# A 3x3 convolution on images kept without a zero border: the centre tap writes every pixel, the other eight add only where a neighbour exists

## The chip, the core and the metric

The kernel runs on one core of a Trainium2 chip. The metric is device time in microseconds (us) of one execution. Before the change three runs gave 1373.08, 1372.49 and 1372.67 us, a median of 1372.67.

## What is computed

The input is 160 images of 128 channels by 32 x 32 pixels. Each image is group-normalised (32 groups of 4 channels), convolved with one of five quantised 3x3 weight sets, and added to itself.

```python
def reference(x, U):
    beta, alpha = jnp.max(U), jnp.min(U)
    s1 = (beta - alpha) / 3.0
    v1 = s1 * floor(U / s1)
    s2 = s1 / 5.0
    v2 = s2 * floor((U - v1) / s2)
    w = (v1 + v2).reshape(128 * 5, 128, 3, 3)
    xb = group_norm(x, groups=32, eps=1e-5).reshape(32, 5 * 128, 32, 32)
    act = conv(xb, w, stride=1, padding=1, feature_group_count=5)
    return x + act.reshape(x.shape)
```

So image 5b + n uses weight set n, and there are 32 images for each of the 5 sets.

## The kernel before

Channels lie on the 128 partitions; an image is one row of 1024 float32 values per partition. Images of one weight set are taken in groups of four (`NB`), one load and one store of 2 MB per group: 40 groups, 160 images. `load` (L288) issues the loads on SyncE's queue, three groups ahead; the stores are issued on ScalarE's queue (L359).

For one group, `statistics` calls `group_statistics` (L126): VectorE takes `bn_stats` of each half image (L135) and `bn_aggr` (L136), a tiny matmul with `gavg` averages over the four channels of a group (L139), VectorE makes the variance, a second tiny matmul averages that (L146), GpSimd raises it to the power -0.5 (L150), and VectorE scales the result (L152).

For one image, `split` (L298) makes the two float16 operands: VectorE normalises into `z` (L302), ScalarE rounds `z` to float16 as `hi` (L311), VectorE subtracts and writes the remainder as `lo` (L312). `hi` and `lo` go into the middle of a padded image of 34 x 34, whose border of zeros was written once: six pairs of such images exist, cleared by GpSimd at the start with 12 memsets (L268).

`conv` (L314) then runs 36 matmuls per image: 9 taps, times `hi` and `lo`, times the two halves of 16 rows. Each streams 16 rows of 32 pixels (512 columns) from the padded image, shifted by the tap, against that tap's 128 x 128 weights, and accumulates in a PSUM tile `pc` of two banks, one per half:

```python
r0 = h * HROWS + kh
nc.tensor.matmul(
    pc[:, h, :].rearrange("p (h w) -> p h w", w=W),
    wt[:, tap, :],
    pair[part][:, r0 : r0 + HROWS, kw : kw + W],
```

A row of the padded image has 34 float16 values (68 bytes), so a tap with `kw` = 1 starts every row on an odd element. VectorE then adds `pc`, scaled, to the image (L332).

`make_weights` (L274) quantises one weight set on VectorE in 17 passes over 1152 values (L87 to L93, L104, L105, L277), transposes the nine taps on TensorE in batches of 4, 4 and 1 (L284), and ScalarE copies each batch to float16 (L285). All quantising needs the global maximum and minimum of U: `Steps` reduces each set on VectorE (L39, L40), then across partitions on GpSimd (L44), and derives the steps in small VectorE operations that begin with `span` (L67).

No order is written out by hand: a scheduler in the framework places the instructions on each engine's queue from its own model of when things are ready, and each engine then runs its queue in that order.

Of the kernel before, what the change touches and what calls it, by code (L numbers as in the profile page):

```python
# [8 lines left out]
F32 = mybir.dt.float32  # L9
I32 = mybir.dt.int32  # L10
MM = mybir.dt.float16
ALU = mybir.AluOpType
# [5 lines left out]
TAPS = 9  # L18
EPS = 1e-5
NB = 4  # L20
# [89 lines left out]
def group_mean_matrix(nc, pool):  # L110

    P = nc.NUM_PARTITIONS
    gavg = pool.tile([P, P // GROUP, GROUP], F32, tag="gavg", name="gavg")
    nc.gpsimd.memset(gavg, 1.0 / GROUP)
    nc.gpsimd.affine_select(
        out=gavg, in_=gavg, compare_op=ALU.is_ge, fill=0.0, base=0,
        pattern=[[-GROUP, P // GROUP], [0, GROUP]], channel_multiplier=1,
    )
    nc.gpsimd.affine_select(
        out=gavg, in_=gavg, compare_op=ALU.is_ge, fill=0.0, base=GROUP - 1,  # L120
        pattern=[[GROUP, P // GROUP], [0, GROUP]], channel_multiplier=-1,
    )
    return gavg.rearrange("p g k -> p (g k)")
# [91 lines left out]
def main_path(tc, keep, x, u, out):  # L215

    nc = tc.nc
    IMGS, C, H, W = x.shape
    P = nc.NUM_PARTITIONS
    assert C == P and H * W == 1024
    PIX = H * W
    HALF = PIX // 2
    HROWS = H // 2  # L230
    FW = C * TAPS
    n_chunks = IMGS // (N_SETS * NB)

    xv = x.rearrange("(b n) c h w -> n c b (h w)", n=N_SETS)
    ov = out.rearrange("(b n) c h w -> n c b (h w)", n=N_SETS)
    uv = u.rearrange("n (o f) -> n o f", o=C)

    ctx = ExitStack()
    const = ctx.enter_context(tc.tile_pool(name="const", bufs=1))
    qpool = ctx.enter_context(tc.tile_pool(name="quant", bufs=1))  # L240
    xpool = ctx.enter_context(tc.tile_pool(name="x", bufs=4))
    zpool = ctx.enter_context(tc.tile_pool(name="z", bufs=2))
    small = ctx.enter_context(tc.tile_pool(name="small", bufs=3))
    ps_conv = ctx.enter_context(tc.tile_pool(name="ps_conv", bufs=3, space=PSUM))
    ps_stat = ctx.enter_context(tc.tile_pool(name="ps_stat", bufs=1, space=PSUM))
    ps_tr = ctx.enter_context(tc.tile_pool(name="ps_tr", bufs=1, space=PSUM))


    us = []
    for n in range(N_SETS):  # L250
        un = const.tile([P, FW], F32, tag=f"u{n}", name=f"u{n}")
        nc.scalar.dma_start(un, uv[n])
        us.append(un)

    ident = const.tile([P, P], F32, tag="ident", name="ident")
    make_identity(nc, ident)
    gavg = group_mean_matrix(nc, const)
    mhalf = const.tile([P, NB], F32, tag="mhalf", name="mhalf")
    nc.gpsimd.memset(mhalf, -0.5)


    N_PADS = 6
    pads = []
    for i in range(N_PADS):
        pair = []
        for part in ("hi", "lo"):
            pad = const.tile([P, H + 2, W + 2], MM, tag=f"{part}{i}", name=f"{part}{i}")
            nc.gpsimd.memset(pad, 0.0)  # L268
            pair.append(pad)
        pads.append(pair)  # L270

    steps = Steps(nc, keep, us)

    def make_weights(n):  # L274

        k1, k2, _ = steps.quantise(qpool, us[n], n)
        nc.vector.scalar_tensor_tensor(k2, k1, 5.0, k2, ALU.mult, ALU.add)  # L277
        wt = const.tile([P, TAPS, C], MM, tag=f"wt{n}", name=f"wt{n}")
        k3 = k2.rearrange("o (i k) -> o i k", k=TAPS)
        for t0 in range(0, TAPS, 4):  # L280
            cnt = min(4, TAPS - t0)
            pt = ps_tr.tile([P, 4, C], F32, tag="pt", name=f"pt{n}_{t0}")
            for k in range(cnt):
                nc.tensor.transpose(pt[:, k, :], k3[:, :, t0 + k], ident)  # L284
            nc.scalar.copy(wt[:, t0 : t0 + cnt, :], pt[:, :cnt, :])  # L285
        return wt

    def load(g):  # L288
        n, c = divmod(g, n_chunks)
        xt = xpool.tile([P, NB, PIX], F32, tag="xt", name=f"xt{g}")  # L290
        nc.sync.dma_start(xt, xv[n, :, c * NB : (c + 1) * NB, :])
        return xt

    def statistics(g, xt):
        images = [xt[:, j, :] for j in range(NB)]
        return group_statistics(nc, small, ps_stat, gavg, mhalf, images, SCALE, g)

    def split(g, j, xt, gm, rstd):  # L298

        hi, lo = pads[(g * NB + j) % N_PADS]  # L300
        z = zpool.tile([P, H, W], F32, tag="z", name=f"z{g}_{j}")
        nc.vector.tensor_scalar(  # L302
            z,
            xt[:, j, :].rearrange("p (h w) -> p h w", w=W),
            gm[:, j : j + 1],
            rstd[:, j : j + 1],
            ALU.subtract,
            ALU.mult,
        )
        hi_in = hi[:, 1 : H + 1, 1 : W + 1]  # L310
        nc.scalar.copy(hi_in, z)  # L311
        nc.vector.tensor_sub(lo[:, 1 : H + 1, 1 : W + 1], z, hi_in)  # L312

    def conv(g, j, xt, wt):  # L314


        pair = pads[(g * NB + j) % N_PADS]
        pc = ps_conv.tile([P, 2, HALF], F32, tag="pc", name=f"pc{g}_{j}")
        for tap in range(TAPS):
            kh, kw = divmod(tap, 3)  # L320
            for part in range(2):
                for h in range(2):
                    r0 = h * HROWS + kh
                    nc.tensor.matmul(  # L324
                        pc[:, h, :].rearrange("p (h w) -> p h w", w=W),
                        wt[:, tap, :],
                        pair[part][:, r0 : r0 + HROWS, kw : kw + W],
                        start=(tap == 0 and part == 0),
                        stop=(tap == TAPS - 1 and part == 1),
                    )  # L330
        xj = xt[:, j, :].rearrange("p (h f) -> p h f", h=2)
        nc.vector.scalar_tensor_tensor(xj, pc, steps.s2z, xj, ALU.mult, ALU.add)  # L332

    total = N_SETS * n_chunks
    ahead = 3
    xts = {g: load(g) for g in range(min(ahead, total))}
    wts = {0: make_weights(0)}
    norm = statistics(0, xts[0])
    split(0, 0, xts[0], *norm)
    split(0, 1, xts[0], *norm)  # L340
    for g in range(total):
        n, c = divmod(g, n_chunks)
        xt = xts.pop(g)
        for j in range(NB):

            if j == 1 and g + 1 < total:
                norm_next = statistics(g + 1, xts[g + 1])
            if j < 2:
                split(g, j + 2, xt, *norm)
            elif g + 1 < total:  # L350
                split(g + 1, j - 2, xts[g + 1], *norm_next)
            conv(g, j, xt, wts[n])
            if j == 0 and g + ahead < total:
                xts[g + ahead] = load(g + ahead)
            if j == 2 and c == 1 and n + 1 < N_SETS:
                wts[n + 1] = make_weights(n + 1)
        if g + 1 < total:
            norm = norm_next
        nc.scalar.dma_start(ov[n, :, c * NB : (c + 1) * NB, :], xt)  # L359
    ctx.close()  # L360
    return steps


@with_exitstack
def preact_conv_kernel(
    ctx: ExitStack,
    tc: tile.TileContext,
    x: bass.AP,
    u: bass.AP,
    out: bass.AP,  # L370
):

    keep = ctx.enter_context(tc.tile_pool(name="keep", bufs=1))
    steps = main_path(tc, keep, x, u, out)
    general_path(tc, keep, steps, x, u, out)
# [28 lines left out]
```

## Time and profile before

| what | us |
|---|---|
| median of 3 runs | 1372.67 |
| the profiled execution, its own time | 1372.45 |
| its span in the trace | 1370.7 |
| TensorE matmul busy | 1294.6 (94%) |
| VectorE busy | 851.3 (62%) |
| ScalarE busy | 168.5 (12%) |
| GpSimd busy | 58.4 (4%) |

A row of the timeline gives the start, the length, the engine, the line and how many instructions were merged; the distance between two starts is the firmer number for matmuls, whose ends are modelled. The table by stage gives each engine's busy time in a stretch. The chain is the sequence of work, each piece released by the one above it, that ended last.

### The profile page before, as it was taken

Reading aid. Unit: us, or ns where it says so; the run is one execution under the profiler, and the core shown is the slowest. Engines: PE = TensorE matmul, PEld = TensorE weight load, DVE = VectorE, ACT = ScalarE, POOL = GpSimd, SP = SyncE. Lnnn points to the kernel's source line nnn. Section 1 sums busy time; section 2 is a strip of 40 time slices with the busy share of each in tenths; the row PEclk is TensorE's granted clock in tenths of the full one; section 3 lists DMA queues with packets and bytes.
Section 4 is the critical chain, followed back from the end, with each engine's and each line's share of the span. In section 5 each row is a group of like instructions: output and inputs, shape, how many; then the busy total and the mean of one; then the engine's idle time right before and its main releaser. Section 6 shows DMA issues by size and latency. Waiting matters only on the chain.

```text
span 1370.7 us, 13928 instructions
## 1 busy us (share of the span) xinstructions
PE 1294.6 (94%) x5965; PEld 584.2 (43%) x5965; DVE 851.3 (62%) x1317; ACT 168.5 (12%) x176; POOL 58.4 (4%) x63
## 2 busy tenths in 40 slices
PE   0199999999999999999999999999999999999997
PEld 0044444444444444444444444444444444444443
DVE  7999975555597666656555555555666665555331
ACT  0201111111111111111111111111111111111110
POOL 4100000000000000000000000000000000000000
PEclk9999999999999999999999999999999999999999
DMA  8003333333433333333333333324333333333221
GB/s 331 0 0 123 123 137 150 143 128 126 174 121 128 123 123 123 123 124 123 123 123 138 150 143 128 152 113 161 123 124 123 123 123 124 123 123 134 89 84 64
DMA packets 43030, 171.69 MB, mean 125 GB/s; under 512 B 1360, under 2 KB 1360, under 8 KB 42960
## 3 DMA queue, kind: packets, MB, share of 16 engines
q1 hardware_dynamic: 21120, 83.89, 16.3%
q10 hardware_dynamic: 21840, 86.84, 15.4%
q8 instruction: 48, 0.79, 0.2%
q14 instruction: 22, 0.18, 0.0%
HBM read 86.84 MB, written 83.89 MB: 125 GB/s over the span
## 4 chain that ended last, share of the span: by engine, by line
PE 86%; DVE 12%; DMA 1%; POOL 0%; issue 0%; ACTq 0%; ACT 0%
PE pc L324 85%; DVE st L135 2%; DVE lo L312 2%; DVE xt L332 1%; DMA u<-in_L_conv_U_dram 1%; DVE z L302 1%; DVE tt L89 1%; DVE tt L91 1%; DVE tt L90 1%; DVE tt L92 1%; DVE k L93 1%; DVE nn L87 0%; DVE k L277 0%; DVE nn L88 0%; PE pg L146 0%; PE pt L284 0%
## 5 line engine op out<-in xcount | busy, mean ns | idle before, releaser
L324 PE MATMUL pc<-hi,wt 128*128 128x512 f16 x2880 | 870.4, 383 | 0.0
L324 PE MATMUL pc<-lo,wt 128*128 128x512 f16 x2880 | 870.3, 383 | 0.0
L324 PEld LDWEIGHTS <-wt 128*128 128x128 f16 x5760 | 561.4, 98 | 692.1 <-issue 2.1
L332 DVE SCALAR_TENSOR_TENSOR xt<-pc,s2z,xt 128x1024 f32<-128x1024 f32 x160 | 204.6, 1279 | 421.0 <-PE pc L324 421.0
L311 ACT CAST hi<-z 128x1024 f16<-128x1024 f32 x160 | 160.2, 1047 | 1079.3 <-DVE z L302 1064.7
L135 DVE BATCH_NORM_STATS2 st<-xt 128x6 f32<-128x512 f32 x320 | 200.5, 666 | 0.0
L312 DVE TENSOR_TENSOR lo<-z,hi 128x1024 f16<-128x1024 f32 x160 | 189.3, 1224 | 16.7 <-ACT hi L311 16.7
L302 DVE TENSOR_SCALAR z<-xt,gm,rstd 128x1024 f32<-128x1024 f32 x160 | 123.1, 809 | 1.3
L150 POOL TENSOR_TENSOR rstd<-ve,mhalf 128x4 f32<-128x4 f32 x40 | 44.1, 1103 | 1239.6 <-DVE ve L148 1230.2
L139 PE MATMUL pg<-mv,gavg 128*128 128x4 f32 x80 | 11.7, 217 | 27.7 <-DVE mv L136 25.9
L284 PE MATMUL pt<-ident,k 128*128 128x128 f32 x45 | 9.2, 318 | 29.6 <-DVE k L277 27.7
L152 DVE TENSOR_SCALAR rstd<-rstd 128x4 f32<-128x4 f32 x40 | 6.8, 170 | 41.9 <-POOL rstd L150 41.9
L136 DVE BATCH_NORM_AGGREGATE mv<-st 128x2 f32<-128x12 f32 x160 | 31.4, 196 | 0.0
L139 PEld LDWEIGHTS pg<-mv,gavg 128*128 128x128 f32 x80 | 15.4, 196 | 33.3 <-issue 25.9
L284 PEld LDWEIGHTS pt<-ident,k 128*128 128x128 f32 x45 | 7.0, 200 | 33.6 <-DVE k L277 27.8
L146 PEld LDWEIGHTS pg<-dv,gavg 128*128 128x128 f32 x80 | 13.9, 194 | 17.1 <-DVE dv L145 17.1
L146 PE MATMUL pg<-dv,gavg 128*128 128x4 f32 x80 | 12.3, 224 | 8.9 <-DVE dv L145 8.9
L148 DVE TENSOR_SCALAR ve<-pg 128x4 f32<-128x4 f32 x40 | 6.5, 162 | 18.3 <-PE pg L146 18.2
L92 DVE TENSOR_TENSOR tt<-tt,nn 128x1152 f32<-128x1152 f32 x10 | 13.5, 1355 | 0.1
L93 DVE TENSOR_TENSOR k<-nn,tt 128x1152 f32<-128x1152 f32 x10 | 13.4, 1345 | 0.1
L39 DVE TENSOR_REDUCE ext<-u 128x1 f32<-128x1152 f32 x5 | 6.8, 1353 | 6.9 <-DMA u<-in_L_conv_U_dram 6.9
L285 ACT CAST wt<-pt 128x512 f16<-128x512 f32 (+1 forms) x15 | 7.2, 479 | 27.4 <-PE pt L284 27.4
(53 smaller groups left out, 127.6 us busy)
## 6 DMA issues: line engine op xcount, KB each, us to landing
xt<-in_x_dram SPq DMA_DIRECT2D x40, 2048.0 KB, 7.5
out_dram<-xt ACTq DMA_DIRECT2D x40, 2048.0 KB, 6.4
u<-in_L_conv_U_dram ACTq DMA_DIRECT2D x5, 576.0 KB, 10.1
```

The source lines that it names most:

```text
L92: nc.vector.tensor_tensor(t, t, n, ALU.is_lt)
L93: nc.vector.tensor_sub(k, n, t)
L135: nc.vector.bn_stats(st[:, h, :], image[:, h * half : (h + 1) * half])
L136: nc.vector.bn_aggr(mv[:, j, :], st)
L139: nc.tensor.matmul(pg[:, 0, :], gavg, mv[:, :, 0], start=True, stop=True)
L146: nc.tensor.matmul(pg[:, 1, :], gavg, dv, start=True, stop=True)
L150: nc.gpsimd.tensor_tensor(rstd, ve, mhalf, ALU.pow)
L302: nc.vector.tensor_scalar(z, xt[:, j, :].rearrange("p (h w) -> p h w", w=W), gm[:, j : j + 1], rstd[:, j : j + 1], ALU.subtract, ALU.mult,)
L311: nc.scalar.copy(hi_in, z)
L312: nc.vector.tensor_sub(lo[:, 1 : H + 1, 1 : W + 1], z, hi_in)
L324: nc.tensor.matmul(pc[:, h, :].rearrange("p (h w) -> p h w", w=W), wt[:, tap, :], pair[part][:, r0 : r0 + HROWS, kw : kw + W], start=(tap ...
L332: nc.vector.scalar_tensor_tensor(xj, pc, steps.s2z, xj, ALU.mult, ALU.add)
```

## The change

The six padded pairs and their memsets are gone. `hi` and `lo` are plain 32 x 32 tiles from a pool of six buffers each. The casts and the subtraction run over 1024 contiguous values. `conv` takes the centre tap first, which writes all 32 x 32 outputs; each other tap reads only the pixels whose shifted neighbour lies inside the image, and adds only to the outputs that have one. A tap that shifts by a row has 31 rows over both halves, and one that shifts by a column has rows of 31 pixels, whose output rows in PSUM are 31 of 32 columns wide.

```diff
-    N_PADS = 6
-    pads = []
...
-            nc.gpsimd.memset(pad, 0.0)
...
+    parts_pool = ctx.enter_context(tc.tile_pool(name="parts", bufs=6))
...
-        hi, lo = pads[(g * NB + j) % N_PADS]
-        z = zpool.tile([P, H, W], F32, tag="z", name=f"z{g}_{j}")
+        z = zpool.tile([P, PIX], F32, tag="z", name=f"z{g}_{j}")
...
+        hi = parts_pool.tile([P, H, W], MM, tag="hi", name=f"hi{g}_{j}")
+        lo = parts_pool.tile([P, H, W], MM, tag="lo", name=f"lo{g}_{j}")
+        hi_flat, lo_flat = (t.rearrange("p h w -> p (h w)") for t in (hi, lo))
+        nc.scalar.copy(hi_flat, z)
+        nc.vector.tensor_sub(lo_flat, z, hi_flat)
+        return hi, lo
...
+    tap_order = [4, 0, 1, 2, 3, 5, 6, 7, 8]
...
-        for tap in range(TAPS):
-            kh, kw = divmod(tap, 3)
+        for tap in tap_order:
+            dh, dw = tap // 3 - 1, tap % 3 - 1
+            c0, c1 = max(0, -dw), W - max(0, dw)
             for part in range(2):
                 for h in range(2):
-                    r0 = h * HROWS + kh
+
+                    r0 = max(h * HROWS, -dh)
+                    r1 = min((h + 1) * HROWS, H - dh)
                     nc.tensor.matmul(
-                        pc[:, h, :].rearrange("p (h w) -> p h w", w=W),
+                        pc[:, h, :].rearrange("p (h w) -> p h w", w=W)[
+                            :, r0 - h * HROWS : r1 - h * HROWS, c0:c1
+                        ],
                         wt[:, tap, :],
-                        pair[part][:, r0 : r0 + HROWS, kw : kw + W],
-                        start=(tap == 0 and part == 0),
-                        stop=(tap == TAPS - 1 and part == 1),
+                        pair[part][:, r0 + dh : r1 + dh, c0 + dw : c1 + dw],
+                        start=(tap == tap_order[0] and part == 0),
+                        stop=(tap == tap_order[-1] and part == 1),
                     )
```

Because the memsets are gone, the scheduler also places the start differently. Line numbers shift: in the changed kernel z is L293, hi L299, lo L300, the last pass of the weights L269, the transposes L276, the weight copies L277, the convolution's matmuls L319, the addition to the image L329.

The first place is VectorE's queue just after the last reduction of U, before the change (st and mv are the statistics of groups 0 and 1, span begins the quantising steps):

```order
L42 TENSOR_REDUCE ext_138<-ext 128x2
L135 BN_STATS st_0_227<-xt_182 128x6
L135 BN_STATS st_1_231<-xt_182 128x6
L136 BN_AGGR mv_226<-st_0_227 128x2
...
L148 TENSOR_SCALAR ve_252<-pg_243 128x4
L136 BN_AGGR mv_309<-st_2_318 128x2
L135 BN_STATS st_3_322<-xt_184 128x6 x2
L67 TENSOR_TENSOR span<-extg 128x1
L78 TENSOR_REDUCE big<-extg 128x1
```

and the same place in the changed kernel:

```order
L42 TENSOR_REDUCE ext_117<-ext 128x2
L135 BN_STATS st_0_206<-xt_161 128x6
L67 TENSOR_TENSOR span<-extg 128x1
L78 TENSOR_REDUCE big<-extg 128x1
L136 BN_AGGR mv_205<-st_0_206 128x2
L49 TENSOR_SCALAR s1q_123<-span 128x1
```

`span` moved from behind the statistics of two groups to behind the first image's first two half-image passes, one of them ahead of these rows.

The second place is VectorE's queue just ahead of the last pass of the first weight set (L277, now L269), before the change (z_0_382 to z_2_467 are images of group 1):

```order
L302 TENSOR_SCALAR z_0_382<-xt_184,gm_328,rstd_337 128x1024
L91 SCALAR_TENSOR_TENSOR tt_189<-tt_189,s2nr,nn_188 128x1152
L312 TENSOR_TENSOR lo_121<-z_0_382,hi_119 128x32x32
L92 TENSOR_TENSOR tt_189<-tt_189,nn_188 128x1152
L302 TENSOR_SCALAR z_1_424<-xt_184,gm_328,rstd_337 128x1024
L93 TENSOR_TENSOR k_0_191<-nn_188,tt_189 128x1152
L312 TENSOR_TENSOR lo_125<-z_1_424,hi_123 128x32x32
L277 SCALAR_TENSOR_TENSOR k_0_191<-k_0_190,k_0_191 128x1152
```

and in the changed kernel:

```order
L91 SCALAR_TENSOR_TENSOR tt_168<-tt_168,s2nr,nn_167 128x1152
L300 TENSOR_TENSOR lo_0_239<-z_0_236,hi_0_238 128x1024
L92 TENSOR_TENSOR tt_168<-tt_168,nn_167 128x1152
L300 TENSOR_TENSOR lo_1_245<-z_1_242,hi_1_244 128x1024
L93 TENSOR_TENSOR k_0_170<-nn_167,tt_168 128x1152
L293 TENSOR_SCALAR z_2_248<-xt_161,gm_224,rstd_233 128x1024
L269 SCALAR_TENSOR_TENSOR k_0_170<-k_0_169,k_0_170 128x1152
```

Before, six images were split ahead of that pass; now two are, with a third one's `z`.

The third place is TensorE's queue at the first image, before (pt are the transposed weights, pc the convolution's accumulator):

```order
L284 MATMUL pt_4_217<-ident,k_0_191 128x128 x4
L324 LDWEIGHTS wt_210
L324 MATMUL pc_0_269<-hi_103,wt_210 128x512
...
L324 MATMUL pc_0_269<-lo_105,wt_210 128x512
L284 MATMUL pt_8_223<-ident,k_0_191 128x128
```

and in the changed kernel:

```order
L276 MATMUL pt_4_196<-ident,k_0_170 128x128 x4
L276 MATMUL pt_8_202<-ident,k_0_170 128x128
L319 LDWEIGHTS wt_189
L319 MATMUL pc_0_254<-hi_0_238,wt_189 128x512
...
L319 MATMUL pc_0_254<-hi_0_238,wt_189 128x15x31
...
L319 MATMUL pc_0_254<-hi_0_238,wt_189 128x16x31
```

All nine transposes now stand ahead of the first convolution matmul, and most of the matmuls after the centre tap have rows of 31.

## Rows read from the trace of the kernel before

**Rows 1.** The page's part 1: busy time, share of the span and instructions of each engine.

```profile
span 1370.7 us, 13928 instructions
PE 1294.6 (94%) x5965; PEld 584.2 (43%) x5965; DVE 851.3 (62%) x1317; ACT 168.5 (12%) x176; POOL 58.4 (4%) x63
```

**Rows 2.** Busy time by stage: stretch, its length, then each engine, clock, DMA.

```profile
0.00:68.00 68.00, 4.71 (x17) 3.73 (x18) 60.86 (x108) 8.17 (x9) 17.91 (x25) 1.00 0.41 167
68.00:100.00 32.00, 32.00 (x139) 13.92 (x138) 30.41 (x38) 2.85 (x4) 0.00 (x0) 1.00 0.00 1
100.00:180.00 80.00, 77.78 (x361) 35.04 (x358) 77.65 (x100) 9.42 (x11) 3.08 (x2) 1.00 0.34 133
180.00:373.00 193.00, 192.86 (x891) 86.81 (x892) 111.27 (x181) 23.96 (x24) 6.04 (x6) 1.00 0.34 133
```

**Rows 3.** Timeline of TensorE, one image: start, length, engine, line, operation.

```profile
605.00 0.59 PE L324 MATMUL pc<-hi,wt 128*128 128x512 f16 x2
...
605.86 0.62 PE L324 MATMUL pc<-hi,wt 128*128 128x512 f16 x2
...
606.77 0.59 PE L324 MATMUL pc<-hi,wt 128*128 128x512 f16 x2
...
608.50 0.62 PE L324 MATMUL pc<-hi,wt 128*128 128x512 f16 x2
...
609.42 0.59 PE L324 MATMUL pc<-hi,wt 128*128 128x512 f16 x2
...
611.16 0.62 PE L324 MATMUL pc<-hi,wt 128*128 128x512 f16 x2
...
612.08 0.59 PE L324 MATMUL pc<-hi,wt 128*128 128x512 f16 x2
...
612.95 0.59 PE L324 MATMUL pc<-hi,wt 128*128 128x512 f16 x2
```

**Rows 4.** The chain in a steady stretch and at the end: start, length, piece.

```profile
244.67 29.60 PE pc L324 x134
...
274.39 2.23 PE pc L324 x10
...
1307.28 53.47 PE pc L324 x242
...
1360.78 1.28 DVE xt L332
```

**Rows 5.** The chain at the start, VectorE's pieces up to the first weights.

```profile
20.61 0.06 DVE ext L42
...
23.12 0.11 DVE mv L136
23.23 1.15 DVE st L135 x2
...
30.82 0.06 DVE span L67
...
49.72 0.72 DVE z L302
...
53.57 1.14 DVE lo L312
...
63.62 1.28 DVE k L277
```

**Rows 6.** Timeline of GpSimd at the start: last memset, all-reduce, first power.

```profile
13.72 1.06 POOL L268 MEMSET lo<- 128x1156 f16 x1
24.46 0.37 POOL L44 PARTITION_ALL_REDUCE extg<-ext  x1 [9.68 <-DVE st L135]
34.20 1.54 POOL L150 TENSOR_TENSOR rstd<-ve,mhalf 128x4 f32<-128x4 f32 x1 [9.37 <-DVE dv L144]
```

**Rows 7.** Timeline at the first image: VectorE's variance, first matmuls, ninth transpose.

```profile
29.39 0.16 DVE L148 TENSOR_SCALAR ve<-pg 128x4 f32<-128x4 f32 x1
...
67.66 1.06 PE L324 MATMUL pc<-hi,wt 128*128 128x512 f16 x2
...
68.94 0.42 PE L284 MATMUL pt<-ident,k 128*128 128x128 f32 x1
```

More of the change, by code (lines that the diff above doesn't have):

```diff
@@ L259, in main_path @@
     nc.gpsimd.memset(mhalf, -0.5)
-    N_PADS = 6
-    pads = []
[L264 to L267, printed above, removed]
-            nc.gpsimd.memset(pad, 0.0)
-            pair.append(pad)
-        pads.append(pair)
+    parts_pool = ctx.enter_context(tc.tile_pool(name="parts", bufs=6))
     steps = Steps(nc, keep, us)
@@ L298, in split @@
     def split(g, j, xt, gm, rstd):
-        hi, lo = pads[(g * NB + j) % N_PADS]
-        z = zpool.tile([P, H, W], F32, tag="z", name=f"z{g}_{j}")
+        z = zpool.tile([P, PIX], F32, tag="z", name=f"z{g}_{j}")
         nc.vector.tensor_scalar(
[L303 to L308, printed above, removed]
-        )
-        hi_in = hi[:, 1 : H + 1, 1 : W + 1]
-        nc.scalar.copy(hi_in, z)
@@ L312, in split @@
-        nc.vector.tensor_sub(lo[:, 1 : H + 1, 1 : W + 1], z, hi_in)
-    def conv(g, j, xt, wt):
-        pair = pads[(g * NB + j) % N_PADS]
+            z, xt[:, j, :], gm[:, j : j + 1], rstd[:, j : j + 1], ALU.subtract, ALU.mult
+        )
+        hi = parts_pool.tile([P, H, W], MM, tag="hi", name=f"hi{g}_{j}")
+        lo = parts_pool.tile([P, H, W], MM, tag="lo", name=f"lo{g}_{j}")
+        hi_flat, lo_flat = (t.rearrange("p h w -> p (h w)") for t in (hi, lo))
+        nc.scalar.copy(hi_flat, z)
@@ L318, in conv @@
+        nc.vector.tensor_sub(lo_flat, z, hi_flat)
+        return hi, lo
+    tap_order = [4, 0, 1, 2, 3, 5, 6, 7, 8]
+    def conv(g, j, xt, wt, pair):
         pc = ps_conv.tile([P, 2, HALF], F32, tag="pc", name=f"pc{g}_{j}")
-        for tap in range(TAPS):
-            kh, kw = divmod(tap, 3)
+        for tap in tap_order:
+            dh, dw = tap // 3 - 1, tap % 3 - 1
+            c0, c1 = max(0, -dw), W - max(0, dw)
             for part in range(2):
                 for h in range(2):
-                    r0 = h * HROWS + kh
+                    r0 = max(h * HROWS, -dh)
+                    r1 = min((h + 1) * HROWS, H - dh)
@@ L338, in main_path @@
     norm = statistics(0, xts[0])
-    split(0, 0, xts[0], *norm)
-    split(0, 1, xts[0], *norm)
+    pairs = [split(0, j, xts[0], *norm) for j in range(2)]
     for g in range(total):
@@ L348, in main_path @@
             if j < 2:
-                split(g, j + 2, xt, *norm)
+                pairs.append(split(g, j + 2, xt, *norm))
             elif g + 1 < total:
-                split(g + 1, j - 2, xts[g + 1], *norm_next)
-            conv(g, j, xt, wts[n])
+                pairs.append(split(g + 1, j - 2, xts[g + 1], *norm_next))
+            conv(g, j, xt, wts[n], pairs.pop(0))
             if j == 0 and g + ahead < total:
```

## The prediction

> **What bounds the kernel now.** I read the page's totals first, then the table by stage, then one image on TensorE, then the chain. The totals show TensorE busy for 94% of the span, VectorE for 62% [rows 1]. By stage there are two regimes: up to 68 us VectorE works alone (60.86 of 68 us) while TensorE has 4.71; from then on TensorE hardly stops: 32.00 of 32, 77.78 of 80 and 192.86 of 193 us, with the clock at full grant [rows 2], which is the level of 2.4 GHz. VectorE is nearly full only up to 180 us. The chain agrees: in a steady stretch it is TensorE alone, 134 convolution matmuls in 29.60 us and 10 in 2.23, and so to the end, where one addition of 1.28 us and the store are left [rows 4]. So each microsecond taken from the convolution matmuls counts, and so does each taken from the start.
>
> The image from 605.00 to 612.95 us has 36 matmuls in 7.95 us; each row merges the two halves of one part, and a tap is two such rows [rows 3]. The middle taps of the three kernel rows (kw = 1) take 0.91, 0.92 and 0.92 us; the other six share 7.95 - 2.75 = 5.20, or 0.867 each, 217 ns per matmul against 512 / 2.4 = 213 ns of columns. A kw = 1 tap costs 0.05 us more for its 64 image rows, 0.8 ns per row. It is the tap that starts every row on an odd float16. Counted in aligned pairs of float16, a row of 32 from an even start touches 16 pairs, from an odd start 17: 17/16 is 6.2% more, and 0.917 / 0.867 is 5.8% more. I take it that the moving operand is fed in pairs.
>
> **The change, part by part.**
>
> *Odd starts.* The centre column's taps now start on even elements: 3 x 0.05 = 0.15 us per image.
>
> *Rows left out.* Six taps shift by a row, and each drops one row in hi and one in lo: 12 rows of 576. A row is 32 / 2.4 = 13.3 ns: 0.16 us per image.
>
> *Columns left out.* Six taps shift by a column; their rows number 2 x 2 x (31 + 32 + 31) = 376 per image, each with 31 columns for 32. The trace has no such row. By columns it saves 0.42 ns, 0.157 us per image. By pairs it saves nothing: 31 values touch 16 pairs from either start. Charging columns, but 0.8 ns for the odd start that half of these rows have, comes to the same within 0.02 ns per row. I take nothing, because the kw = 1 rows are the nearest, and keep 0.157 as the far end. In the other direction there is the output, now 31 of 32 columns, a form no row shows; its bounds are among the rivals. Together 0.31 us per image, 160 images: **-49.6 us**.
>
> [...]
>
> *Start.* The memsets (12, the last at 13.72 us) go from GpSimd. VectorE's queue now does less ahead of the first weights: from the order, 7 half-image statistics, 4 aggregations, 3 z, 4 lo and some 6 tiny operations move behind them. By the chain's steps (1.15 for two statistics, 0.11, 0.72, 1.14, 0.08 estimated from the tiny ones) this is 4.0 + 0.4 + 2.2 + 4.6 + 0.5 = 11.7 us [rows 5]. Against that, VectorE now waits for the first power, about 0.9 us (its 1.54 [rows 6] and a hand-over, less one pass in between such as the 0.72 of z), and the centre tap needs the second weight copy, with the ninth transpose in front of it: 68.94 - 67.66 = 1.3 us [rows 7]. That leaves -9.5 us if GpSimd is ready in time. Whether it is, the trace does not decide. The all-reduce shows at 24.46, which is 9.68 us after the last memset's end, and 3.8 after its input at 20.67; the first power starts at 34.20, 9.37 after the all-reduce, and 4.65 after its input at 29.55 [rows 5 to 7]. If 9.5 us run from the previous GpSimd work, both are ready early once the memsets are gone. If 3.8 and 4.65 us follow the input, `span`, which stood at 30.82 and so hid the wait, now waits 3.7 us and the power 4.6 more: -9.5 + 8.3 = -1.2 us. I take the middle, **-5.5 us**, with both ends kept.
>
> [...]
>
> *Work moved behind the start.* The 11.7 us of VectorE's work now falls where it is busiest, 77.65 of 80 us [rows 2]. What gives way there is the quantising of later weight sets, needed only 32 images, some 254 us, apart; so most of it stays hidden. But the tiny matmuls of the statistics wait for VectorE, and between the two of them TensorE now has 10 shorter matmuls (2.23 us before [rows 4]; about 2.13 after, by the terms above), some 0.1 us less cover in each of 39 groups. I charge **+3 us**; nothing at one end, and 11.7 if all of the moved work comes back as waits.
>
> *At nothing.* Contiguous casts and subtractions run beside TensorE: ScalarE's 168.5 and VectorE's 851.3 us are far from the bound [rows 1], and without that cover the whole subtraction, 1.14 us per image, is slower work only in the first 180 us. Loads, stores, and the number of buffers (six pairs) are as before.
>
> **Sum.** Against the profiled execution, 1372.45 us (its span is 1370.7; the median of the runs is 0.2 higher): 1372.45 - 49.6 - 5.5 + 3 = **1320 us**.
>
> **The rivals.**
>
> *Columns count.* TensorE gains by the column, at 2.4 columns per ns, whatever the start: 0.157 x 160 = 25 us more, **1295 us**. For it: the even taps run at 217 ns for 512 columns. Against: the kw = 1 taps.
>
> *A broken row costs a step.* Each of the 376 rows per image pays what an odd start pays, 0.8 ns on top of 13.3, because its output is not contiguous: 376 x 0.8 x 160 = 48 us back, **1368 us**. For it: input and output of these rows are shifted by one against each other. Against: the kw = 1 rows are shifted too, and pay no more than the 17th pair.
>
> *The narrow rows write PSUM badly: slower.* If two columns leave the array together and land in two aligned words of PSUM, each such pair needs two writes. For all pairs of the 376 rows that doubles 13.3 ns: 376 x 13.3 x 160 = 800 us, 2120 us; for half the pairs **1720 us**. It decides from 53 us / (160 x 376) = 0.88 ns per row on. For it: every matmul of the trace writes PSUM without a gap, so nothing here excludes it. Against: if pairs kept the input's alignment, the kw = 1 taps would straddle already, and they lose only 0.8 ns per row.
>
> [...]
>
> That the change doesn't do what it says is hardly open: the order shows 15 x 31 and 16 x 31 where 512 stood.
>
> **How the numbers follow.** The forecast 0.53, columns count 0.17, a broken row costs a step 0.13, slower 0.15, and 0.02 for no effect. No change means within 0.2%, 2.7 us, about what a measurement of this kernel can tell. The broken row's price lies so close to break-even that 0.02 of its chance fall within and 0.02 beyond: faster 0.53 + 0.17 + 0.09 = 0.79, same 0.04, slower 0.17. The range takes in the columns with the better start, 1295 - 4 - 3 = 1288, and the broken row, to 1369; it leaves out the slow case.
>
> **What would show it.** Right: an image of about 7.64 us on TensorE, all taps without a row shift at 0.86 to 0.87 us, whatever their column shift, the others near 0.84. Columns count: the taps with 31 columns at 0.84 and 0.81. Broken row: 0.91 and 0.89. Slow: 1.3 us and more. For the start: the first convolution matmul near 58 us and the all-reduce right behind its input, or near 66 and again 4 us behind it; 62 would be the middle. I am wrong if the taps with 31 columns differ by the direction of their shift, or if TensorE shows more than 3 us of new waits between 60 and 200 us.

## The result and the profile after

The changed kernel takes 1316.04 us (median of four runs, 1315.41 to 1317.36) where the kernel before takes 1372.58 in the runs beside it: a ratio of 0.959, with a 95% interval from 0.9573 to 0.9606. The profiled execution took 1316.06 us, its span is 1314.3 us. The forecast was 1320, in a range from 1288 to 1369.

The page's first part, of the changed kernel:

```profile
span 1314.3 us, 13910 instructions
PE 1243.5 (95%) x5965; PEld 585.9 (45%) x5965; DVE 853.1 (65%) x1317; ACT 168.0 (13%) x176; POOL 47.6 (4%) x51
```

TensorE's busy time fell by 51.1 us, the span by 56.4; VectorE's busy time is nearly what it was, 853.1 us against 851.3 [rows 1]. One image of the changed kernel on TensorE; of the centre tap and of taps 0, 3, 5, 6, 7 and 8 the first of their two rows stands here, then the next image's first. Merged rows show the columns of the first matmul in them:

```profile
702.23 0.59 PE L319 MATMUL pc<-hi,wt 128*128 128x512 f16 x2
...
703.09 0.58 PE L319 MATMUL pc<-hi,wt 128*128 128x465 f16 x2
...
705.60 0.60 PE L319 MATMUL pc<-hi,wt 128*128 128x496 f16 x2
...
706.47 0.60 PE L319 MATMUL pc<-hi,wt 128*128 128x496 f16 x2
...
707.33 0.58 PE L319 MATMUL pc<-hi,wt 128*128 128x496 f16 x2
...
708.17 0.58 PE L319 MATMUL pc<-hi,wt 128*128 128x512 f16 x2
...
709.01 0.58 PE L319 MATMUL pc<-hi,wt 128*128 128x496 f16 x2
...
709.85 0.59 PE L319 MATMUL pc<-hi,wt 128*128 128x512 f16 x2
```

The order is centre, then taps 0, 1, 2, 3, 5, 6, 7, 8. The centre tap takes 0.86 us, and so do taps 3 and 5, which have 31 columns and all rows: 0.87 and 0.86. The six taps that leave out a row take 0.84: taps 0, 1 and 2 have 2.51 us together, and 6, 7 and 8 have 0.84 each, whether their rows have 31 columns (0, 2, 6, 8) or 32 (1 and 7). The image takes 7.62 us against 7.95 [rows 3], and no tap stands at 0.92 any more. The left-out columns show nowhere.

The last two pieces of TensorE in the chain of the changed kernel:

```profile
1250.22 2.14 PE pc L319 x10
...
1252.53 51.26 PE pc L319 x242
```

The last 242 matmuls took 53.47 us before [rows 4], 220.95 ns each; now 51.26 us, 211.82 ns each. Over 5760 matmuls that is 52.6 us.

The start, in the timeline of the changed kernel:

```profile
21.55 0.14 DVE L42 TENSOR_REDUCE ext<-ext 128x2 f32<-128x10 f32 x1
...
21.83 0.37 POOL L44 PARTITION_ALL_REDUCE extg<-ext  x1 [19.01 <-DVE ext L42]
...
40.31 0.15 DVE L148 TENSOR_SCALAR ve<-pg 128x4 f32<-128x4 f32 x1
...
40.63 1.48 POOL L150 TENSOR_TENSOR rstd<-ve,mhalf 128x4 f32<-128x4 f32 x1 [18.43 <-DVE ve L148]
...
59.06 1.06 PE L319 MATMUL pc<-hi,wt 128*128 128x512 f16 x2
```

Both GpSimd operations now follow their input at once, by 0.14 and 0.17 us; before, 3.8 and 4.65 us lay between [rows 6, 7]. The first convolution matmul stands at 59.06, 8.6 us earlier than at 67.66 [rows 7], although the last set of U was reduced 1.0 us later here than before (the last L40 starts at 19.69, before at 18.66). The first image takes 2.0 us more than a later one in both kernels (9.91 us against 7.95, and 9.60 against 7.62), because its first matmuls are slow: the row at 59.06 has two in 1.06 us, later rows have two in about 0.6. So that is no part of the difference.

The table by stage, of the changed kernel (columns as in [rows 2]):

```profile
90.00:170.00 80.00, 78.83 (x380) 37.20 (x378) 77.96 (x106) 9.30 (x11) 3.68 (x2) 1.00 0.36 140
170.00:230.00 60.00, 57.67 (x277) 27.08 (x277) 48.02 (x69) 8.07 (x8) 2.58 (x2) 1.00 0.34 131
```

TensorE is idle for 1.2 and 2.3 us between 90 and 230 us, where it was idle for 2.2 us between 100 and 180 and 0.1 between 180 and 373 before [rows 2].

### The profile page after: what moved, and what is told of

Its sections match the earlier page's. It is cut to its first block, busy times and chain, and to the rows that moved or that the text cites. A ratio compares the mean times of both kernels' runs of the same rounds, so it can differ in the third digit from the quotient of the medians.

```text
span 1314.3 us, 13910 instructions
## 1 busy us (share of the span) xinstructions
PE 1243.5 (95%) x5965; PEld 585.9 (45%) x5965; DVE 853.1 (65%) x1317; ACT 168.0 (13%) x176; POOL 47.6 (4%) x51
## 4 chain that ended last, share of the span: by engine, by line
PE 82%; DVE 15%; DMA 1%; POOL 1%; issue 0%; ACTq 0%; ACT 0%; POOLq 0%
PE pc L319 81%; DVE st L135 2%; DVE xt L329 2%; DVE lo L300 2%; DVE z L293 1%; DMA u<-in_L_conv_U_dram 1%; DVE tt L89 1%; DVE k L93 1%; DVE tt L91 1%; DVE tt L90 1%; DVE tt L92 1%; POOL rstd L150 1%; PE pg L146 0%; DVE nn L88 0%; DVE nn L87 0%; DVE k L269 0%
## 5 line engine op out<-in xcount | busy, mean ns | idle before, releaser
L319 PEld LDWEIGHTS <-wt 128*128 128x128 f16 x5760 | 565.5, 99 | 636.7 <-issue 2.4
L319 PE MATMUL pc<-lo,wt 128*128 128x496 f16 (+3 forms) x2880 | 846.3, 376 | 0.0
L319 PE MATMUL pc<-hi,wt 128*128 128x496 f16 (+3 forms) x2880 | 846.2, 376 | 0.0
L329 DVE SCALAR_TENSOR_TENSOR xt<-pc,s2z,xt 128x1024 f32<-128x1024 f32 x160 | 204.4, 1278 | 362.0 <-PE pc L319 362.0
L299 ACT CAST hi<-z 128x1024 f16<-128x1024 f32 x160 | 159.7, 1043 | 1066.4 <-DVE z L293 1066.4
L300 DVE TENSOR_TENSOR lo<-z,hi 128x1024 f16<-128x1024 f32 x160 | 188.6, 1219 | 15.8 <-ACT hi L299 15.8
L293 DVE TENSOR_SCALAR z<-xt,gm,rstd 128x1024 f32<-128x1024 f32 x160 | 122.8, 808 | 1.2
L152 DVE TENSOR_SCALAR rstd<-rstd 128x4 f32<-128x4 f32 x40 | 6.8, 170 | 43.5 <-POOL rstd L150 43.5
L276 PE MATMUL pt<-ident,k 128*128 128x128 f32 x45 | 9.5, 326 | 17.6 <-DVE k L269 15.5
L146 PE MATMUL pg<-dv,gavg 128*128 128x4 f32 x80 | 13.7, 242 | 9.5 <-DVE dv L145 9.5
L146 PEld LDWEIGHTS pg<-dv,gavg 128*128 128x128 f32 x80 | 12.2, 191 | 20.8 <-DVE dv L145 20.7
L276 PEld LDWEIGHTS pt<-ident,k 128*128 128x128 f32 x45 | 7.0, 199 | 21.7 <-DVE k L269 15.6
L277 ACT CAST wt<-pt 128x512 f16<-128x512 f32 (+1 forms) x15 | 7.2, 478 | 23.1 <-PE pt L276 23.1
```

The source lines that it names most:

```text
L146: nc.tensor.matmul(pg[:, 1, :], gavg, dv, start=True, stop=True)
L293: nc.vector.tensor_scalar(z, xt[:, j, :], gm[:, j : j + 1], rstd[:, j : j + 1], ALU.subtract, ALU.mult)
L299: nc.scalar.copy(hi_flat, z)
L300: nc.vector.tensor_sub(lo_flat, z, hi_flat)
L319: nc.tensor.matmul(pc[:, h, :].rearrange("p (h w) -> p h w", w=W)[:, r0 - h * HROWS : r1 - h * HROWS, c0:c1], wt[:, tap, :], pair[part][:, ...
```

## Experiments

Two questions stood behind a forecast that held: is the theory of pairs the reason that 31 columns cost as much as 32, and what did the start gain? The theory was that the moving operand is fed in aligned pairs of float16, and that the output's place does not matter. Rivals: columns count; or a broken row costs just what its column saves.

### The picture one column further right

```diff
-pad = const.tile([P, H + 2, W + 2], ...)
+pad = const.tile([P, H + 2, W + 4], ...)
-hi_in = hi[:, 1 : H + 1, 1 : W + 1]
+hi_in = hi[:, 1 : H + 1, 2 : W + 2]    # lo likewise
-pair[part][:, r0 : r0 + HROWS, kw : kw + W]
+pair[part][:, r0 : r0 + HROWS, kw + 1 : kw + 1 + W]
```

> The kernel before, with the padded images 36 wide and the picture one column further right, so that the left and right taps start on odd elements and the middle ones on even. Theory (an odd start costs one pair more per row): the slow taps are 0, 2, 3, 5, 6 and 8 at 0.92 us, and 1, 4 and 7 fall to 0.865; three slow taps more, 3 x 0.055 x 160 = 26 us, 1399 us. Rival (the middle taps are slow for another reason, their weights or their place in the sequence): they stay at 0.92, and the time stays at 1373 us.

It took 1395.71 us, 1.0169 times the kernel before (1.0154 to 1.0185), 22.8 us more. Taps 0, 1 and 2 of one image of this kernel:

```profile
744.26 0.62 PE L324 MATMUL pc<-hi,wt 128*128 128x512 f16 x2
...
745.18 0.59 PE L324 MATMUL pc<-hi,wt 128*128 128x512 f16 x2
...
746.04 0.62 PE L324 MATMUL pc<-hi,wt 128*128 128x512 f16 x2
```

Tap 0 takes 0.92 us and tap 1 0.86; of tap 2 the two halves of one part take 0.62, as those of tap 0. Slow is what starts on an odd element, not the middle column. This part of the theory is shown. The time came 3 us short of the 1399 expected.

### Whole rows as one run

```diff
-pair[part][:, r0 + dh : r1 + dh, c0 + dw : c1 + dw]
+flat[:, s + lo_cut : e - hi_cut]    # s = (r0 + dh) * W + dw
```

The output is the same run of `pc`, 32 columns per row.

> The changed kernel, but taps that shift by a column read and write whole rows as one run of the flat image (32 columns per row, with the neighbour row's pixel at the edge, so the border column is not the convolution's). Rows are left out as in the change. Theory (pairs: leaving out a column saves nothing): the same time as the changed kernel, 1316 us within 2, the taps at 0.84 and 0.865 us. Rival (columns count, 0.42 ns each): 376 columns per image come back, 25 us more, 1341 us. Rival (broken rows cost what the column saves): 1316 as well; the run with other widths tells that one.

It took 1321.7 us (ratio to before 0.9627, 0.9613 to 0.964), 5.7 more than the changed kernel and 19 less than if columns counted. Taps 3 and 5 of one image of it:

```profile
709.16 0.60 PE L323 MATMUL pc<-hi,wt 128*128 128x511 f16 x2
...
710.03 0.60 PE L323 MATMUL pc<-hi,wt 128*128 128x512 f16 x2
```

Tap 3 takes 0.87, with 32 columns per row (but for the image's corner): what the changed kernel's takes with 31. "Columns count" falls. The image takes 7.65 us, 0.03 more, or 4.8 us in all, which the theory does not have. The odd starts account for a part of it at most: 16 matmuls of an image have an even number of columns and start on an odd element, and at 0.8 ns each, what an odd start costs per row in the next run (0.05 us for 64), I estimate 13 of the 30 ns. Where the rest comes from stays open.

### Other windows

```diff
-dh, dw = tap // 3 - 1, tap % 3 - 1
-c0, c1 = max(0, -dw), W - max(0, dw)
+wd, ci, co = WIN[tap]
...
+pc[:, h, :].rearrange("p (h w) -> p h w", w=W)[:, :, co : co + wd]
+pair[part][:, r0:r1, ci : ci + wd]
```

> Each of the eight outer taps gets its own window over all 16 rows of a half, so the sums are not the convolution: tap 0 reads columns 0-29 and writes 0-29, tap 1 reads 1-30 and writes 0-29, tap 2 reads 0-29 and writes 1-30, tap 3 reads 1-30 and writes 1-30, tap 5 is 31 wide from 1 to 1, tap 6 is 31 wide from 0 to 0, tap 7 is 29 and tap 8 is 28 wide from 0. Times are for the four matmuls of a tap. Theory (the moving operand is fed in aligned pairs of float16, the place of the output does not matter): tap 0 and tap 2 at 0.81 us, tap 1 and tap 3 at 0.865, tap 5 and tap 6 at 0.865, tap 7 at 0.81, tap 8 at 0.76; the whole kernel about 1299 us. Rival (the pairs are those of the output in PSUM): tap 0 and tap 1 at 0.81, tap 2 and tap 3 at 0.865, the rest alike. Rival (a column is 0.42 ns, and each broken row costs 0.42 ns besides, so that 31 columns only happen to cost as much as 32): all four 30-wide taps at 0.84, tap 8 at 0.785; the whole about 1303 us.

One image of this kernel, from tap 0 on, in the order 0, 1, 2, 3, 5, 6, 7, 8:

```profile
700.59 0.57 PE L319 MATMUL pc<-hi,wt 128*128 128x480 f16 x2
...
701.40 0.59 PE L319 MATMUL pc<-hi,wt 128*128 128x480 f16 x2
...
702.26 0.59 PE L319 MATMUL pc<-hi,wt 128*128 128x480 f16 x2
...
703.12 0.62 PE L319 MATMUL pc<-hi,wt 128*128 128x480 f16 x2
...
704.03 0.60 PE L319 MATMUL pc<-hi,wt 128*128 128x496 f16 x2
...
704.90 0.60 PE L319 MATMUL pc<-hi,wt 128*128 128x496 f16 x2
...
705.77 0.57 PE L319 MATMUL pc<-hi,wt 128*128 128x464 f16 x2
...
706.58 0.54 PE L319 MATMUL pc<-hi,wt 128*128 128x448 f16 x2
...
707.34 0.59 PE L319 MATMUL pc<-hi,wt 128*128 128x512 f16 x2
```

| width, read from, written from | measured us per tap | steps per row |
|---|---|---|
| 30, 0, 0 | 0.81 | 15 |
| 30, 1, 0 | 0.86 | 16 |
| 30, 0, 1 | 0.86 | 16 |
| 30, 1, 1 | 0.91 | 17 |
| 31, 1, 1 and 31, 0, 0 | 0.87 | 16 |
| 29, 0, 0 | 0.81 | 15 |
| 28, 0, 0 | 0.76 | 14 |

A step is 0.83 ns, the time of two columns. The next run gives it: there three taps of 480 columns per matmul in one run take 2.44 us (627.67 to 630.11), or 0.813 each, and one of 256 takes 0.44, so 4 x 224 columns are 0.373 us: 0.417 ns per column, 2.4 columns per ns (the granted clock of that run is 0.998, of this one 0.997). Of the 0.813 us this leaves 13 ns, some 3 per matmul. With both, 64 rows of 15, 16 or 17 steps come to 0.81, 0.865 and 0.92 us. The rival of a price per broken row falls: 30 columns from 0 to 0 take 0.81, not 0.84. The rival that the pairs are those of the output alone falls too: it had 0.81 for a read from 1, which takes 0.86. But the theory is not whole either: it had 0.81 for a write from 1, and 0.865 for the window odd on both sides. At this even width an odd start of the output costs as much as one of the input (0.86 us each, against 0.81), and the two add up (0.91). The whole took 1313.19 us, not 1299, for that reason.

### Runs and steps

```diff
+0: (o[:, 0:480], a[:, 0:480]),     1: (o[:, 0:480], a[:, 1:481]),
+2: (o[:, 1:481], a[:, 0:480]),     3: (o[:, 0:256], a[:, 0:256]),
+5: (o2[:, :, 0], a[:, 0:256]),     6: (o2[:, :, 1], a[:, 0:256]),
+7: (o[:, 0:256], a2[:, :, 0]),     8: (o2[:, :, 0], a2[:, :, 0]),
```

(`o` is a half of `pc`, `a` a half image as one row, `o2` and `a2` the same in steps of two; the output comes first.)

> The outer taps stream runs and steps of one float16 row without the shifts of the convolution, so the sums are not the convolution: tap 0 480 columns in one run from 0 to 0, tap 1 the same read from 1, tap 2 the same written from 1, tap 3 256 columns in one run, tap 5 256 columns written to every second column from 0, tap 6 written to every second column from 1, tap 7 256 columns read from every second element, tap 8 every second element on both sides. Times are for the four matmuls of a tap. Theory (pairs of the input, output free): taps 0, 1, 2 at 0.81 us, taps 3, 5, 6 at 0.44, taps 7 and 8 at 0.865 because each element then needs a pair of its own; the whole about 1115 to 1125 us. Rival (PSUM is written in aligned words of two float32, and a pattern with gaps pays for each word): tap 2 slower than tap 1, taps 5 and 6 at 0.865 or more; the whole about 1250 us or more.

One image of this kernel, from tap 0 to tap 8:

```profile
627.67 0.57 PE L328 MATMUL pc<-hi,wt 128*128 128x480 f16 x2
...
628.48 0.57 PE L328 MATMUL pc<-hi,wt 128*128 128x480 f16 x2
...
629.30 0.57 PE L328 MATMUL pc<-hi,wt 128*128 128x480 f16 x2
...
630.11 0.38 PE L328 MATMUL pc<-hi,wt 128*128 128x256 f16 x2
...
630.55 0.59 PE L328 MATMUL pc<-hi,wt 128*128 128x256 f16 x2
...
631.37 0.64 PE L328 MATMUL pc<-hi,wt 128*128 128x256 f16 x2
...
632.23 0.43 PE L328 MATMUL pc<-hi,wt 128*128 128x256 f16 x2
...
632.73 0.59 PE L328 MATMUL pc<-hi,wt 128*128 128x256 f16 x2
```

A run of 480 read from 1 takes 0.82 us, one written from 1 0.81, one from 0 to 0 0.81: the odd start of a whole run is too little to see, so it is the 16 rows that make it dear. 256 columns take 0.44 us; written with a step of two, 0.82 and 0.86, twice as much; read with a step of two, 0.50. Of this 0.50 the first two matmuls, right behind the slow output of tap 6, have 0.27, and the other two, which start at 632.50, have 0.23, hardly more than the 0.22 of two matmuls of tap 3. So the theory fails for the input, where elements out of two different aligned pairs go nearly as fast as neighbours. The rival is right for a stepped output, where the time is that of one step per column, but tap 2 is not slower than tap 1, as it had expected. The whole, 1175.8 us, lies between the two sums.

### A third set, for the revised rule

```diff
+WIN = {4: (32, 0, 0), 0: (26, 1, 1), 1: (29, 1, 1), 2: (30, 1, 1), 3: (30, 2, 1), 5: (30, 1, 2)}
...
+mov = flat.rearrange("p (f s) -> p f s", s=4)[:, :, 0]            # tap 6
+mov = flat[:, 0:1023].rearrange("p (f s) -> p f s", s=3)[:, :, 0]  # tap 7
+dst = pc[:, h, 0:510].rearrange("p (f s) -> p f s", s=3)[:, :, 0]  # tap 8
```

> As in the run with other windows, the outer taps are not those of the convolution. Windows as (width, first column read, first column written), 16 rows each: tap 0 (26, 1, 1), tap 1 (29, 1, 1), tap 2 (30, 1, 1), tap 3 (30, 2, 1), tap 5 (30, 1, 2). Tap 6 reads 256 elements with a step of 4, tap 7 341 with a step of 3, tap 8 writes 170 columns with a step of 3. Times are for the four matmuls of a tap. Revised theory (a row takes half its columns, rounded up, in steps of 0.83 ns; with an even width an odd start of the input adds one step, an odd start of the output another, and the two add up): tap 0 0.81 us, tap 1 0.81, tap 2 0.92, tap 3 0.865, tap 5 0.865. Rival (the larger of the aligned pairs touched on either side): tap 0 0.76, tap 1 0.81, taps 2, 3, 5 0.865. For steps of the input: if two elements are taken at once when they lie in the same 8 bytes, tap 6 0.865 and tap 7 0.865; if in the same 16 bytes, tap 6 0.44 and tap 7 0.72; if steps are free, 0.44 and 0.58. For the output: if each column written with a step takes a step of its own, tap 8 0.58; if free, 0.44 or less, where the weight loads set the pace.

One image of this kernel, from tap 0 on:

```profile
686.94 0.57 PE L331 MATMUL pc<-hi,wt 128*128 128x416 f16 x2
...
687.74 0.57 PE L331 MATMUL pc<-hi,wt 128*128 128x464 f16 x2
...
688.55 0.62 PE L331 MATMUL pc<-hi,wt 128*128 128x480 f16 x2
...
689.46 0.60 PE L331 MATMUL pc<-hi,wt 128*128 128x480 f16 x2
...
690.33 0.60 PE L331 MATMUL pc<-hi,wt 128*128 128x480 f16 x2
...
691.19 0.62 PE L331 MATMUL pc<-hi,wt 128*128 128x256 f16 x2
...
692.09 0.63 PE L331 MATMUL pc<-hi,wt 128*128 128x341 f16 x2
...
693.01 0.45 PE L331 MATMUL pc<-hi,wt 128*128 128x170 f16 x2
...
693.54 0.64 PE L331 MATMUL pc<-hi,wt 128*128 128x512 f16 x2
```

Taps 0, 1, 2, 3 and 5 take 0.80, 0.81, 0.91, 0.87 and 0.86 us: the revised rule gives all five, the rival misses (26, 1, 1) and (30, 1, 1). Taps 6 and 7, the steps of four and three on the input, take 0.90 and 0.92, near the 0.865 of "two at once if in the same 8 bytes", some 0.04 above it. Tap 8 takes 0.53, near the 0.58 of one step per column. That weight loads would set the pace of short matmuls was an estimate, and no run shows it (a load takes 98 ns on average in the kernel before, 561.4 us for 5760). The readings by 16 bytes (0.44 and 0.72) and of free steps (0.44 and 0.58) fall; the 8 bytes are the nearest of the three. The rule describes the forms tried; how the engine comes to it, the runs do not tell.

### The memsets back, all and half

```diff
+for i in range(12):    # 6 in the second kernel
+    cleared = const.tile([P, H + 2, W + 2], MM, ...)
+    nc.gpsimd.memset(cleared, 0.0)
```

> The changed kernel, with the 12 memsets of 1156 values back on GpSimd, into tiles that nothing reads. The order ahead of the first weights is then that of before: 19 half-image statistics, 6 z, 6 lo. Theory (GpSimd needs some 9.7 us from its previous work to the all-reduce, and the scheduler puts span behind other work to cover it): all-reduce at 24.5 us, first convolution matmul near 68.5 us, and 7 to 9 us more than the changed kernel, 1323 to 1325 us. Rival (the start was gained by the contiguous casts and subtractions, or the moved work comes back later as waits): no more than 2 us, 1316 to 1318 us.

With twelve it took 1323.4 us (ratio to before 0.9639, 0.9626 to 0.9652), 7.4 us more than the changed kernel. Its timeline at the start:

```profile
24.45 0.37 POOL L44 PARTITION_ALL_REDUCE extg<-ext  x1 [9.66 <-DVE st L135]
...
69.04 1.06 PE L322 MATMUL pc<-hi,wt 128*128 128x512 f16 x2
```

The all-reduce is back at 24.45, and the first matmul at 69.04, 1.4 us behind the kernel before. Of this, 1.15 us is the centre tap's wait for the second weight copy, with the ninth transpose in front: from the first transpose to the first convolution matmul it is 3.87 us here (from 65.17) and 2.72 before (from 64.94).

> The same with six memsets; the last ends near 8.5 us. Ahead of the first weights stand 15 half-image statistics, 3 z and 3 lo, 3.1 us more work than in the changed kernel. Theory (9.7 us run from the last GpSimd work): 8.5 + 9.7 = 18.2 us lies before the input of the all-reduce, so it follows its input at once, near 21.5 us, and the first convolution matmul stands at 61 to 62 us; 1318 to 1320 us. Rival (3.8 us follow the input whenever memsets stand ahead): the all-reduce near 25 us.

With six it took 1316.38 us (ratio 0.9588, 0.9575 to 0.9602), no more than the changed kernel. Its timeline:

```profile
21.08 0.14 DVE L42 TENSOR_REDUCE ext<-ext 128x2 f32<-128x10 f32 x1
21.36 0.38 POOL L44 PARTITION_ALL_REDUCE extg<-ext  x1 [12.59 <-DVE ext L42]
...
61.76 1.06 PE L322 MATMUL pc<-hi,wt 128*128 128x512 f16 x2
```

The all-reduce follows its input by 0.14 us, with 12.59 us behind GpSimd's previous work, and the first power follows its own by 0.16, with 12.62. So the delay is not one that follows the input: it runs from GpSimd's previous work and can lie beside VectorE's. Its length is not one number. Where it shows, the all-reduce stands 9.66 to 10.14 us behind the last memset and the first power 8.09 to 9.43 us behind the all-reduce (the kernel before, the run with twelve memsets, and the run with the picture further right, which has the 10.14 and the 8.09). What fills that time, no run shows.

The first matmul stands at 61.76, as expected, yet the time is not 2 to 4 us longer. The medians are 0.3 us apart, with intervals of some 2 us to either side; of the profiled executions, this one's span is 1.1 us longer (1315.4 against 1314.3), where its start is 2.7 us later. So most of the last 2.7 us of the start was worth nothing. The later start has more of VectorE's work done, and TensorE waits less afterwards:

```profile
170.00:230.00 60.00, 59.88 (x288) 28.05 (x287) 46.61 (x69) 8.16 (x8) 2.58 (x2) 1.00 0.36 139
```

0.1 us of idle TensorE, against 2.3 in the changed kernel; from 90 to 170 us it is 1.7 against 1.2.

### The start alone

```diff
-nc.gpsimd.memset(pad, 0.0)
+nc.vector.memset(pad, 0.0)
```

> The kernel before, with only the 12 memsets moved from GpSimd to VectorE, which has nothing to do before the first set of U arrives; padded images and matmuls as before. Theory (the start and the matmuls are separate gains): the first convolution matmul at 58 to 61 us, an image still 7.95 us, and 6 to 9 us less than before, 1364 to 1367 us. Rival (the start is worth nothing, because the moved work comes back as waits): 1372 us.

It took 1363.68 us, 0.9931 of the kernel before (0.9917 to 0.9944), 9.1 us less with the convolution untouched: an image still takes 7.95 us. The first matmul:

```profile
57.64 1.06 PE L324 MATMUL pc<-hi,wt 128*128 128x512 f16 x2
```

It stands 10.0 us earlier than before. So one word is worth a sixth of the whole gain. With the twelve memsets back, the other side was measured: the new matmuls with the old start gain 1372.82 - 1323.4 = 49.4 us. Together 58.5, of which the changed kernel keeps 56.5.

### z on ScalarE

```diff
-nc.vector.tensor_scalar(z, xt[:, j, :], gm[:, j : j + 1], rstd[:, j : j + 1], ALU.subtract, ALU.mult)
+nc.scalar.activation(z, xt[:, j, :], ...Identity, bias=gm[:, j : j + 1], scale=rstd[:, j : j + 1])
...
+nc.vector.scalar_tensor_tensor(shift, gm, -1.0, rstd, ALU.mult, ALU.mult)
+return shift, rstd
```

`statistics` now returns `shift`, which is -gm times rstd, in the place of gm, so the `gm` in the first added line is that shift: one small VectorE operation per group.

> The changed kernel, with z made by ScalarE (x times rstd plus a shift that VectorE makes once per group) in place of VectorE: 160 operations of 0.81 us leave VectorE, 20 or so of them in the first 230 us. Theory (up to some 230 us VectorE's total work sets the pace, so that the later start of the run with six memsets cost nothing): the first convolution matmul 1 to 2 us earlier and most of the 3.5 us of TensorE's waits between 90 and 230 us gone, 1310 to 1313 us. Rival (those waits come from the order of the statistics in VectorE's queue, not from the amount of work): 1315 to 1316 us. Slower if ScalarE's longer chain from rstd to hi delays the first images: 1317 us or more.

> The changed kernel itself, on the same chip and beside the same runs of the kernel before as the version with z on ScalarE: 1316 us within 1.5.

On the same chip it took 1314.19 us (1313.86 to 1314.72, ratio to before 0.9573, 0.956 to 0.9586) and the changed kernel 1316.41 (0.9589, 0.9576 to 0.9602): 2.2 us less. The five times of the one lie all below the five of the other, so the gain is there, though smaller than expected: it falls between the 1310 to 1313 of the theory and the 1315 to 1316 of the rival, and neither holds as put. The first matmul stands 0.6 us earlier (58.49 against 59.08), and the first 20 images take 1.4 us less (160.5 against 161.9). Its table from 170 to 230 us:

```profile
170.00:230.00 60.00, 58.98 (x285) 27.90 (x286) 32.83 (x57) 17.02 (x16) 2.48 (x3) 1.00 0.33 129
```

VectorE has 15 us less to do there, but TensorE still waits for 1.0 us, and from 90 to 170 us for 1.2, as in the changed kernel. What TensorE waits for from 170 to 230 us is the second statistics matmul's input (L146, for VectorE's `dv`, L145): two waits of 2.3 us together in the changed kernel, one of 1.3 here. That fits the rival, by which the place of the statistics in VectorE's queue makes the wait; it is not shown, since no run changed that order alone.

## Why the prediction held, point by point

**Odd starts and rows left out.** The steps came as put: no tap at 0.92, the taps without a row at 0.83 to 0.84. The 2.4 of the prediction is borne out by the runs as a rate: 0.417 ns per column, 2.4 columns per ns, at a granted clock of 0.998. The term was -49.6 us; by the chain it is -52.6. The difference is 19 ns per image, and the steps of 10 ns in the rows that I read the taps from allow that: an odd start was read as 0.05 us per tap, and three taps at 0.055 are 15 ns more.

**Columns left out.** That they save nothing was right: 496 columns take as long as 512, the matmuls of taps 3 and 5 216 ns each, those of the centre tap 215. The reason given was right only in part. "Charging columns, but 0.8 ns for the odd start" came to the same, and hid that the output has a price as well. The windows showed that at an even width input and output each add a step for an odd start (30 columns: 0.81, 0.86 and 0.91 us per tap); the steps showed that "the moving operand is fed in pairs" of aligned float16 is wrong: elements in steps of two go almost as fast as neighbours (0.50 us against 0.44).

**The slow rival** did not come. Its 0.88 ns per row was the point to watch: a window that is even in width and odd on both sides costs 1.6 ns per row more than one that starts even on both (0.91 us against 0.81 for 64 rows of 30 columns). This change's windows have 31 columns, where both odd starts are free (0.87 us from 1 to 1 and from 0 to 0). The prediction put the output at nothing for want of a row; that this came out was luck, for it did not know that the odd width decides it. That two aligned words of PSUM need two writes was this rival's assumption, and no run shows it as such. An output in steps of two takes twice the time (256 columns: 0.82 and 0.86 us against 0.44), rows with a gap of one column do not (496 columns: 216 ns, 512: 215).

**Start.** The middle value, -5.5 (exactly it is -5.35), was too small. The first matmul came 8.6 us earlier, and 9.6 if the later U is left out, which is the better of the two ends (-9.5). I took the middle because the two readings of GpSimd's delay could not be told apart; the six memsets tell them apart. Where there is idle time ahead, the traces show no delay behind the input: with 12.59 or 19.01 us of it, the all-reduce follows its input by 0.14 us.

**Work moved behind the start.** Charged with 3 us; by difference 52.6 + 8.6 - 56.4 = 4.8 us came back. The first matmul of the 21st image, before and after, shows where:

```profile
234.09 0.59 PE L324 MATMUL pc<-hi,wt 128*128 128x512 f16 x2
...
220.63 0.60 PE L319 MATMUL pc<-hi,wt 128*128 128x512 f16 x2
```

The first 20 images take 166.4 us before and 161.6 after, 4.9 less; at 0.329 us per image (9.13 ns for each of 36 matmuls) it would be 6.6. So 1.7 us came back there, where the moved work falls; the sign of being wrong, more than 3 us of new waits between 60 and 200 us, did not come. The other 140 images, to the end of the last matmul, take 1126.7 and 1083.2 us, 43.5 less for 46.0: another 2.5 us, long after the start. Most of it fits what this term also named, the shorter cover between the two statistics matmuls. The chain's piece between them and the last one, before:

```profile
1304.93 2.23 PE pc L324 x10
```

It ends at 1307.16, and the last piece starts at 1307.28 [rows 4]: 0.12 us lie between them, and 0.17 in the changed kernel (1250.22 + 2.14, then 1252.53): 0.05 us in each group, 1.7 us in the last 34, where the prediction had 0.1. The remaining 0.8 us are the same wait once more, for `dv` (L145) in images 41 to 44: 1.3 us after, 0.5 before. The last 0.5 of the 4.8 us lie behind the last matmul, in the addition and the store (10.5 us against 10.0). That each microsecond taken from the start counts was too much said: the run with six memsets had a start 2.7 us later at hardly any cost.

So 1320 against 1316.04: two gains were sized 3.0 and 3.1 us too small, and the loss 1.8 us too small. The mechanism of the start and of the rows was the one that was named; that of the columns, aligned pairs on the input alone, was not.

## What to carry to other kernels

When rows of a matmul's window are short (here 26 to 32 float16 columns, written to float32), count steps of two columns per row (0.83 ns each here), rounded up, and one more for each side that starts on an odd element with an even width: an edge column left out may be free of cost and free of gain, while moving the rows to an even start was worth 0.05 us per tap here. When an engine's first call of a new kind stands 8 to 10 us behind its previous work, look at what stands ahead of it on its queue: twelve small memsets into tiles that nothing reads cost 7.4 us, because the order of the start moved with them. And where two engines are both full, a part of an earlier start can be given back as waits; the run with six memsets started 2.7 us later and took 1316.38 us, where the changed kernel took 1316.04 and, in its second set of runs, 1316.41.

## What was not expected

With an even width, an odd start of the output costs the same 0.8 ns per row as one of the input, and the two add up (30 columns: 0.81, 0.86 and 0.91 us per tap). A step of two on the input costs little (0.50 us for 4 x 256 columns, against 0.44, and 0.05 of the 0.06 falls to the two matmuls right behind the slow tap before), a step of two on the output doubles the time (0.82 and 0.86). Whole rows as one run, the form with the fewest starts, were not the fastest: 7.65 us per image against 7.62.
